# Two graph layers in one kernel: planned PSUM banks, and attention scores in clusters of four

## The chip, the cores and the metric

The kernel runs on one core of a Trainium2 chip. The metric is the device time of one execution in microseconds (us), the median of several runs. All arithmetic is float32. Engines are named as in the profile: PE is TensorE, DVE is VectorE, ACT is ScalarE, POOL is GpSimd, and SP is SyncE, whose queue issues nearly all DMAs.

## The reference

Two layers follow each other on 64 graphs of 256 nodes with 512 features. `adj` is the same 0/1 matrix in both.

```python
# layer 0
fp = x @ fc_w.T + fc_b
logits = (fp @ q_w.T + q_b) + swap(fp @ k_w.T + k_b)     # one number per pair of nodes
masked = logits + (1 - adj) * -1e9
masked = where(masked >= 0, masked, 0.01 * masked)
x = softmax(masked) @ fp + x
# layer 1, 8 heads of 64
Q, K, V = x @ W_q + b_q, x @ W_k + b_k, x @ W_v + b_v
scores = Q K^T / sqrt(64) + (x @ w_g[:D])[:, None] + (x @ w_g[D:])[None, :] + b_g + log(adj + 1e-9)
out = softmax(scores) @ V + x
```

## The kernel before

**Groups and steps.** Two graphs make a group: 512 nodes in four tiles of 128. There are 32 groups. `step(d, a, f, n, check)` runs once per group, and interleaves up to four groups at different stages: F (`f`) goes through layer 0 and the projections of layer 1, A (`a`, one group earlier) through the attention of layer 1, D (`d`, one earlier still) is finished and stored, and X (`n`, the next) is loaded. The schedule is written out by hand: strings such as `A("scores:2 attend:0 totals_0")` name methods of a group, and each method puts its instructions on the engines' queues in that order. Every engine works through its own queue in order, and waits by semaphore for what its operands need. In `attention_and_layer_0` (L1068) stands the first half of a step, in `step` (L1107) the second. The first group's layer 0 is computed on a path of its own (`features_first`), and the last step has no next group and runs the last group's attention too.

**Products.** Each projection (`pq`, `pk`, `pv`, and `pf` for layer 0) is a 2x2 block product with seven multiplications instead of eight, as in Strassen's scheme. `p1` to `p7` are those; each is four matmuls of 128x128 by 256 columns (`Product.add`, L401, matmul at L412), and the profile counts two instructions for a float32 matmul. Some open a PSUM bank (`fresh`: p1, p7, p2, and for `pf` p3), some add to one that stands (p6, p5, p3 to p1's; p4 to p7's). `keep_1` and others copy a bank to SBUF on ACT (L429, L432, L494), and `sum_00`, `sum_11`, `sum_10` add such a copy to a bank on DVE (L443, L501). So pk.p4 may add to its bank only when DVE has read it for pk.sum_11.

**Attention.** `scores:u` (L847) makes two blocks of scores, u being a graph of the group and half of its heads. A block is four matmuls with 64 rows each (L859); two of them use the upper and lower half of the array at the same time, and write two banks. One exponential on ACT reads both banks of the block, 1024 elements per partition (L873). `factor:u:jc` multiplies a block by the adjacency on DVE (L879), `both:u` adds the two blocks (L886), `parts:u` makes row sums of them. `attend:gr` (L888) multiplies the weights by V with 64 columns per matmul (L899), `totals` sums over partitions with a short matmul (L927). `turn`, `ratios`, `divide`, `complete`, `store` finish the output on DVE and send it off.

**Layer 0 and the loads.** `mix:c` (L689) multiplies x by the weights of layer 0. `send`/`fetch` bring the new x through DRAM into transposed form by one DMA out and four DMAs in; `xsum` (L375) and `copy` (L378) prepare sums and copies of its blocks. `keys:t` takes a dot product of each tile of x (L519, named `jc`); x has one buffer, so `load_x` for the next group can start only after that, and `dot_q`, `dot_k` (L519, `jq` and `jk`) wait for that load. `weights:jc` (L604 to L609) makes the next group's layer 0 weights.

**PSUM.** There are eight banks of 128x512 float32. Pool `ps` has four one-bank buffers that rotate over all uses (`bank(name)`), pool `psc` has two pairs of banks (`pair(name)`), for score blocks and for pq.p7. A tile waits until the last reader of the buffer that it gets is done.

Of the kernel before, what the change touches and what calls it, by code (L numbers as in the profile page):

```python
# [17 lines left out]
P = 128  # L18
# [7 lines left out]
def kernel(  # L26
# [118 lines left out]

    def transposed_weights(w, pool, psum, copy):

        t = pool.tile([P, NC, D], F32, tag="fcT", name="fcT")
        for hc in range(NC):
            pt = psum.tile([P, 512], F32, tag="bank", name=f"pfc_{hc}")  # L150
            for oc in range(NC):
                nc.tensor.transpose(pt[:, ts(oc, P)], w[:, oc, ts(hc, P)], ident)
            copy(t[:, hc, :], pt)
        return t
# [9 lines left out]
    def fast():  # L164
        main = ExitStack()
        with main:
# [5 lines left out]
            ps = main.enter_context(  # L172
                tc.tile_pool(name="ps", bufs=4, space=bass.MemoryType.PSUM)
            )
            psc = main.enter_context(
                tc.tile_pool(name="psc", bufs=2, space=bass.MemoryType.PSUM)
            )

            def bank(name):
                return ps.tile([P, 512], F32, tag="bank", name=name)  # L180

            def pair(name):
                return psc.tile([P, 2, 512], F32, tag="pair", name=name)

# [60 lines left out]
            def columns(rows, cols, name):  # L245

                n = rows.shape[0]
                pt = bank(name)
                nc.tensor.transpose(pt[:, 0:n], rows, ident[0:n, 0:n])
                nc.vector.tensor_copy(cols, pt[:, 0:n])  # L250
# [6 lines left out]
            def rows_of_x():  # L257

                pr = bank("rows_qk")[0:2, :]
                for oc in range(NC):  # L260
                    nc.tensor.matmul(
                        pr, lhsT=cols_0[:, oc : oc + NC + 1 : NC], rhs=fc_nat[:, oc, :],
                        start=(oc == 0), stop=(oc == NC - 1),
                    )
                rows = one.tile([2, D], F32, tag="junk", name="rows_qk_sb")
                nc.scalar.copy(rows, pr)
                return rows

            def spread_rows(rows):

                for n, dst in enumerate((wq_row, wk_row)):
                    pt = bank(f"row_{n}")
                    nc.tensor.matmul(
# [5 lines left out]
            def constant():  # L279
# [5 lines left out]
                nc.vector.tensor_reduce(part[:, 0, 0:1], both, AX.X, ALU.add)  # L285
                pk = bank("pk")
                nc.tensor.matmul(
# [7 lines left out]
            def constants_of_projections():  # L295


                pc = bank("pc")[:, 0:HALF]
                for c in range(NC):
# [10 lines left out]
                def add():  # L310
                    pt = bank("pct")
                    for m in range(2):
# [76 lines left out]
            class Product:  # L389
# [4 lines left out]

                scores = False

                def __init__(self, name, a, b, out, rows, bias=None):
                    self.name, self.a, self.b, self.out = name, a, b, out
                    self.rows, self.bias = rows, bias

# [16 lines left out]

                def fresh(self, n, scores=False):
                    name = f"{self.name}_{n}"
                    dst = (pair(name)[:, 0] if scores else bank(name)).rearrange(  # L420
                        "p (m k) -> p m k", m=2
                    )
                    self.add(n, dst, True)
                    return dst
# [36 lines left out]
                def p7(self):  # L461
                    self.r2 = self.fresh(7, self.scores)

# [65 lines left out]
            class Group:  # L529


                older = None

                def __init__(self, g):
# [42 lines left out]
                def queries(self):  # L577

                    pt = bank(f"qrow_{self.g}")
                    for t in range(T):  # L580
# [51 lines left out]
                def recip(self):  # L632

                    lo = ALL - TOK // B
                    first = lo if self.older is None else 0
                    all_sums = bank(f"rc_{self.g}")[:, 0:ALL]
                    nc.tensor.matmul(  # L637
# [14 lines left out]
                def sums(self):  # L652

                    sm = bank(f"sm0_{self.g}")[:, 0:P]
                    for jc in range(TPG):
# [9 lines left out]
                def recip_of_sums(self):  # L665
                    pt = bank(f"rc_{self.g}")[:, 0:P]
                    nc.tensor.transpose(pt, self.sms, ident)
# [4 lines left out]
                def mix(self, c):  # L672

                    g = self.g
                    if c == 0:
# [9 lines left out]
                        )  # L685
                    y = bank(f"y_{g}_{c}")
                    for gr in range(GP):
# [9 lines left out]
                def features_first(self):  # L697
# [4 lines left out]
                    for t in range(T):  # L702
                        pt = bank(f"xTp_{g}_{t}")
                        for c in range(NC):
# [4 lines left out]
                        if t == 0:  # L709
                            spread_rows(rows_qk)  # L710
                    fcT = transposed_weights(fc_nat, wts, ps, nc.scalar.copy)
                    for t in range(T):
                        self.dot_q(t)

                    def product(t):
                        pp = bank(f"fp_{g}_{t}")
                        for c in range(NC):
# [28 lines left out]
                    for t in range(T):  # L746
                        gr, ic = divmod(t, TPG)
                        po = bank(f"x1p_{g}_{t}")
                        for j in range(TPG):
# [15 lines left out]
                def begin(self):  # L765
# [18 lines left out]
                    self.pq = Product(f"pq_{g}", "q", b, to(self.qT), False, bq_col)  # L784
                    self.pq.scores = True
                    self.pk = Product(f"pk_{g}", "k", b, to(self.kT), False)
# [20 lines left out]
                def x1t(self, t):  # L807

                    pt = bank(f"x1Tp_{self.g}_{t}")
                    for c in range(NC):  # L810
# [36 lines left out]
                def scores(self, u):  # L847
# [5 lines left out]
                    for jc in range(TPG):  # L853
                        t = gr * TPG + jc
                        sc = pair(f"sc_{g}_{u}_{jc}").rearrange("p a (b i) -> p a b i", b=2)
                        for pr in range(2):
                            for par in range(2):
                                rows = slice(par * HD, (par + 1) * HD)
                                nc.tensor.matmul(  # L859
                                    sc[:, par, pr, :],  # L860
                                    lhsT=self.kT[rows, 2 * hg + pr, ts(t, P)],
# [9 lines left out]
                        else:  # L871
                            e = six.tile([P, 2, 2, N], F32, tag="e", name=f"e_{g}_{u}_{jc}")
                        nc.scalar.activation(e, sc, AF.Exp, bias=self.c[:, t : t + 1], scale=SCALE)  # L873
                        self.e[u, jc] = e
# [13 lines left out]
                def attend(self, gr):  # L888
# [3 lines left out]
                    for hg in range(2):  # L892
                        po = bank(f"oT_{g}_{gr}_{hg}")
                        oT = po.rearrange("p (r i) -> p r i", r=2)
# [39 lines left out]
                def totals_1(self):  # L934
                    self.totals(1, bank(f"tot_{self.g}_1")[:, 0 : NC * N // B])

                def totals_0(self):
                    self.totals(0, bank(f"tot_{self.g}_0")[:, 0 : NC * N // B])

# [15 lines left out]
                def sums_1(self, gr):  # L955

                    g = self.g

                    sm = bank(f"sm_{g}_{gr}")[:, 0:N]
                    for hg in range(2):  # L960
# [10 lines left out]
                def sums_of_e(self, gr):  # L971

                    g = self.g
                    sm = bank(f"sm_{g}_{gr}")[:, 0:N]
                    for hg in range(2):
# [92 lines left out]
            def attention_and_layer_0(D, A, F, X):  # L1068

                A("scores:0")  # L1070
                D("attend:1")
                F("add_tiles")
                A("scores:1 factor:0:0 factor:0:1 pv.sum_11 pv.p3 pv.p4")
                D("turn:1")
                F("parts_0")
                A("factor:1:0 factor:1:1 pv.sum_10 both:0 both:1")
                F("mix:0 mix:1 ysum:0 recip")
# [6 lines left out]
                F("pf.p7 pf.p5 pf.p3 pf.add_01 pf.sum_11 send:1:1")  # L1084
                A("scores:2 attend:0 totals_0")
                F("pf.sum_01 send:0:1 fetch:1:1 fetch:0:1")
                F("copy:0")
                A("factor:2:0 factor:2:1 scores:3 turn:0 ratios:0 both:2")
                F("pf.p4 pf.sum_10 send:1:0 fetch:1:0")
                F("pq.p1 pq.keep_1 pk.p1 pk.keep_1 pv.p1 pv.keep_1")  # L1090

            def check_ranges():

                in_range(NG - NR // 2, NG, "last")
                pk = bank("pok")
                nc.tensor.transpose(pk[0:1, 0:P], checked["all"], ident)
# [10 lines left out]
            def step(d, a, f, n, check):  # L1107
# [23 lines left out]
                F("xsum:0 xsum:1 xsum:2 pq.p6")  # L1131
                A("factor:3:0 factor:3:1 both:3")
                F("keys:2 keys:3 keys:0 keys:1")
# [16 lines left out]
                F("turn_residual:0")  # L1150
                if n is None:
                    A("attend:1 totals_1 ratios:1 turn:1 divide:1 complete:1 store:1")
                    F("residual:1 turn_residual:1")
# [16 lines left out]
            with tc.manual_schedule(engines=ENGINES):  # L1170
                f = Group(0)
                f.x, f.a = x_0, adj_0

                warm = bank("warm")
                for n in range(6):
# [16 lines left out]
    def general(pool):  # L1192
# [12 lines left out]
        with tc.tile_pool(name="gwps", bufs=2, space=bass.MemoryType.PSUM) as wps:  # L1205
            fcT = transposed_weights(fc_nat, pool, wps, nc.vector.tensor_copy)
        with tc.For_i(0, NG, 1) as g, ExitStack() as stack:
# [198 lines left out]
```

## Time and profile before

| | |
|---|---|
| Median of three runs | 2311.59 us (2310.92 to 2312.35) |
| Profiled execution, first to last instruction (its span) | 2308.8 us |
| Median less span | 2.8 us |
| Mean granted TensorE clock | 0.997 of full |
| PE instructions | 12618 |
| One steady step | 70.88 us |
| PE, DVE, ACT busy in one steady step (70.90 us window) | 70.90, 66.35, 33.42 us |

The profile gives the span of its one execution, and no other time of it. The median less the span is what lies around the instructions. A row of the profile's groups reads: line, engine, operation, output and inputs by name, shape, number of instructions, then busy time, mean duration in ns, and idle time before them. "64*128" at a matmul is the part of the array in use: rows by columns.

### The profile page before, as it was taken

To read this page: it belongs to the slowest core of one execution; us is meant where nothing else is said; L and a number is where in the kernel's file an instruction comes from. 1 tells how busy PE (TensorE), PEld (TensorE's weight loads), DVE (VectorE), ACT (ScalarE), POOL (GpSimd) and SP (SyncE) were. 2 spreads that over 40 slices of the span, in tenths; PEclk is the share of its full clock that TensorE was granted. 3 is DMA by queue.
4 is the path that set the end of the run, shared out by engine and by line. 5 is a ranking of instruction groups with operands and counts; after the bars stand their busy time and mean duration, and the time that the engine had idled before them with its cause. 6 is when DMAs were issued, how large, how long until landed. Compare 5 with 4: busy or idle time off the path is not lost.

```text
span 2308.8 us, 33613 instructions
## 1 busy us (share of the span) xinstructions
PE 2294.2 (99%) x12618; PEld 1905.2 (83%) x12618; DVE 2124.2 (92%) x3180; ACT 1071.8 (46%) x1865; POOL 121.9 (5%) x120
## 2 busy tenths in 40 slices
PE   9999999999999999999999999999999999999997
PEld 6888888888888888888888888888888888888885
DVE  6899999999999999999999999999999999999997
ACT  3544444454445444454444454444544445444443
POOL 0000000000000000000000000000000000000000
PEclk9999999999999999999999999999999999999999
DMA  4122332223322233232233232332222323223312
GB/s 133 46 61 73 78 76 66 70 61 85 79 73 61 61 78 78 74 68 61 69 78 83 60 75 63 79 78 74 64 60 74 78 73 70 65 64 81 84 46 38
DMA packets 517264, 163.84 MB, mean 71 GB/s; under 512 B 415188, under 2 KB 478696, under 8 KB 517096
## 3 DMA queue, kind: packets, MB, share of 16 engines
q1 hardware_dynamic: 514440, 160.32, 28.8%
q8 instruction: 102, 1.67, 0.3%
q10 hardware_dynamic: 2656, 1.31, 0.2%
q14 instruction: 66, 0.54, 0.1%
HBM read 95.43 MB, written 66.12 MB: 70 GB/s over the span
## 4 chain that ended last, share of the span: by engine, by line
PE 98%; DVE 1%; DMA 0%; ACT 0%; issue 0%; ACTq 0%; DVEq 0%
PE pv L412 17%; PE pq L412 17%; PE pf L412 16%; PE pk L412 16%; PE sc L859 11%; PE oT L899 10%; PE y L689 9%; PE fp L718 1%; DMA fc_nat<-in_L_gnn_fc_w_dram 0%; PE rc L637 0%; DVE osb L1034 0%; PE tot L927 0%; DVE osb L1040 0%; PE xTp L705 0%; DVE osb L1033 0%; DVE x L756 0%
## 5 line engine op out<-in xcount | busy, mean ns | idle before, releaser
L873 ACT ACTIVATE e<-sc,c 128x1024 f32<-128x1024 f32 x254 | 269.0, 1110 | 79.2 <-PE sc L859 77.6
L879 DVE TENSOR_TENSOR e<-e,am 128x1024 f32<-128x1024 f32 x254 | 297.7, 1213 | 0.4 <-ACT e L873 0.4
L859 PE MATMUL sc<-qT,kT 64*128 64x256 f32 x2048 | 255.8, 390 | 0.3 <-ACT e L873 0.3
L899 PE MATMUL oT<-e,v 128*64 128x256 f32 x2032 | 233.4, 382 | 0.0
L859 PEld LDWEIGHTS sc<-qT,kT 64*128 64x128 f32 x2048 | 187.3, 187 | 52.6 <-issue 32.7
L495 POOL TENSOR_TENSOR pf_s<-pf_s,x 128x512 f32<-128x512 f32 x93 | 118.4, 1273 | 2106.1 <-ACT pf_s L494 2038.8
L689 PE MATMUL y<-e,x 128*128 128x256 f32 x992 | 225.6, 381 | 0.0
L899 PEld LDWEIGHTS oT<-e,v 128*64 128x64 f32 x2032 | 140.2, 137 | 85.3 <-issue 10.7
L689 PEld LDWEIGHTS y<-e,x 128*128 128x128 f32 x992 | 186.4, 190 | 23.7
L432 ACT ACTIVATE pq_s<-pq,cols 128x256 f32<-128x256 f32 x192 | 80.5, 470 | 249.1 <-PE pq L412 249.1
L494 ACT ACTIVATE pf_s<-pf,recip 128x256 f32<-128x256 f32 x186 | 77.9, 470 | 197.6 <-PE pf L412 197.6
L917 DVE TENSOR_REDUCE part<-est 128x32 f32<-128x1024 f32 x124 | 151.3, 1220 | 4.3
L916 DVE STREAM_TRANSPOSE est<-es 128x1024 f32<-128x1024 f32 x124 | 152.2, 1227 | 0.0
L886 DVE TENSOR_TENSOR es<-e,e 128x1024 f32<-128x1024 f32 x126 | 149.3, 1205 | 1.1
L695 ACT COPY yT<-y 128x512 f32<-128x512 f32 x124 | 72.6, 585 | 131.7 <-PE y L689 130.9
L429 ACT COPY pk_s<-pk 128x512 f32<-128x512 f32 x96 | 56.3, 586 | 165.7 <-PE pk L412 159.0
L906 ACT COPY oTs<-oT 128x512 f32<-128x512 f32 x128 | 75.0, 586 | 118.0 <-PE oT L899 97.3
L412 PE MATMUL pk<-t1b,wk 128*128 128x256 f32 x512 | 121.1, 380 | 0.4 <-DVE kT L443 0.4
L412 PE MATMUL pv<-wv,t1b_c 128*128 128x256 f32 x512 | 121.1, 380 | 0.0
L412 PE MATMUL pv<-wv,t1b 128*128 128x256 f32 x512 | 121.0, 380 | 0.0
L412 PE MATMUL pq<-x1T,wq 128*128 128x256 f32 x512 | 121.0, 379 | 0.0
L412 PE MATMUL pk<-x1T,wk 128*128 128x256 f32 x512 | 121.0, 379 | 0.0
(181 smaller groups left out, 4506.3 us busy)
## 6 DMA issues: line engine op xcount, KB each, us to landing
x<-in_x_dram SPq DMA_DIRECT2D x32, 1024.0 KB, 5.1
out_dram<-osb SPq DMA_DIRECT2D x254, 128.0 KB, 3.1
xd<-xt SPq DMA_DIRECT2D x124, 256.0 KB, 2.0
x1T<-xd SPq DMA_DIRECT2D x496, 64.0 KB, 1.9
adj<-in_adj_dram SPq DMA_DIRECT2D x128, 128.0 KB, 3.5
qrow<-q SPq DMA_DIRECT2D x31, 256.0 KB, 3.9
fc_nat<-in_L_gnn_fc_w_dram ACTq DMA_DIRECT2D x4, 256.0 KB, 3.8
wq<-in_L_gnn_W_q_dram SPq DMA_DIRECT2D x1, 1024.0 KB
```

What stands on the lines that cost most here:

```text
L412: nc.tensor.matmul(o, lhsT=lk[:, ts(m, P)] if len(lk.shape) == 2 else lk[:, m], rhs=rk, start=(start and m == 0 and k == 0), stop=(m == 1 ...
L432: nc.scalar.activation(dst[:, m], src[:, m], AF.Identity, bias=self.bias[:, 2 * o + m : 2 * o + m + 1],)
L494: nc.scalar.mul(s[:, m], src[:, m], self.recip[:, TPG * k + m : TPG * k + m + 1])
L495: nc.gpsimd.tensor_tensor(s, s, self.out(o, k), ALU.add)
L689: nc.tensor.matmul(y[:, ts(gr, N)], lhsT=self.x[:, gr * TPG + j, ts(c, P)], rhs=self.e0[:, j, gr, :], start=(gr == 0 and j == 0), stop=(gr ...
L859: nc.tensor.matmul(sc[:, par, pr, :], lhsT=self.kT[rows, 2 * hg + pr, ts(t, P)], rhs=self.qT[rows, 2 * hg + pr, ts(gr, N)], start=True, st ...
L873: nc.scalar.activation(e, sc, AF.Exp, bias=self.c[:, t : t + 1], scale=SCALE)
L879: nc.vector.tensor_tensor(ef, ef, self.am[:, jc, u // 2, :].unsqueeze(1).to_broadcast([P, 4, N]), ALU.mult,)
L886: nc.vector.tensor_tensor(self.esum[u], self.e[u, 0], self.e[u, 1], ALU.add)
L899: nc.tensor.matmul(oT[par * HD : (par + 1) * HD, pr, :], lhsT=self.v[:, gr * TPG + jc, ts(h, HD)], rhs=self.e[2 * gr + hg, jc][:, par, pr, :],
L916: nc.vector.transpose(turned, self.esum[u].rearrange("p a b i -> p (a b i)"))
L917: nc.vector.tensor_reduce(self.part[:, hg, :], turned.rearrange("p (m c) -> p m c", c=B), AX.X, ALU.add,)
```

## The change

Eight PSUM tiles of one bank each, named Xa, Xb, Ya, Yb, Za, Zb, Wa and Wb, take the place of both pools. Every product of a projection gets a fixed slot. Score blocks of a step use pairs: Y, Z, W, Y for `scores:0` and `scores:1`, and X, Z, W, X for `scores:2` and `scores:3`; attention, totals and row sums have slots too. The last group keeps to Y and Z. What has no slot of its own takes seven of the banks in turn. The two banks of a block are now separate tiles, and each is read by an exponential of its own, 512 elements per partition.

The order of a step changes in `attention_and_layer_0`: `attend:1` of the older group goes ahead of `scores:0`, `scores:1` follows `scores:0` at once, and pf.p4 moves between `totals_0` and `scores:2`, with `scores:3` as the next matmuls. On VectorE, `parts_0` and the turning of outputs move with it, and `factor:2:0` is issued after the first products of pq, pk and pv; `factor:2:1` and `both:2` move into the second half of the step, behind the first three `xsum`.

```diff
+            banks = {
+                n + h: ps.tile([P, 512], F32, tag=f"bank_{n}{h}", name=f"bank_{n}{h}")
+                for n in "XYZW" for h in "ab"
+            }
+            FREE = ("Xa", "Xb", "Ya", "Yb", "Za", "Zb", "Wa")
+            def bank(slot=None):
+                if slot is None:
+                    turns[0] += 1
+                    slot = FREE[turns[0] % len(FREE)]
+                return banks[slot]
...
+                slots = dict(v="Xa Xb Wb", q="Ya Yb Wa", k="Za Zb Ya", fc="Xa Yb Xb Za")
...
+                score_pairs = "YZWYXZWX"
+                attend_slots = 2 * (("Wa", "Wb"),)
+                total_slots = ("Ya", "Zb")
+                sum_slots = ("Wb", "Xa")
...
-                        nc.scalar.activation(e, sc, AF.Exp, bias=self.c[:, t : t + 1], scale=SCALE)
+                        for par in range(2):
+                            nc.scalar.activation(
+                                e[:, par], sc[par], AF.Exp, bias=self.c[:, t : t + 1], scale=SCALE
+                            )
...
-                A("scores:0")
                 D("attend:1")
-                F("add_tiles")
-                A("scores:1 factor:0:0 factor:0:1 pv.sum_11 pv.p3 pv.p4")
+                F("add_tiles parts_0")
+                A("scores:0 scores:1 pv.sum_11")
                 D("turn:1")
-                F("parts_0")
-                A("factor:1:0 factor:1:1 pv.sum_10 both:0 both:1")
+                A("factor:0:0 factor:0:1 pv.p3 pv.p4 factor:1:0 both:0 factor:1:1 pv.sum_10 both:1")
...
-                A("scores:2 attend:0 totals_0")
+                A("attend:0 totals_0")
                 F("pf.sum_01 send:0:1 fetch:1:1 fetch:0:1")
-                F("copy:0")
-                A("factor:2:0 factor:2:1 scores:3 turn:0 ratios:0 both:2")
-                F("pf.p4 pf.sum_10 send:1:0 fetch:1:0")
+                F("pf.p4")
+                A("ratios:0 turn:0 scores:2")
+                F("pf.sum_10 send:1:0 fetch:1:0 copy:0")
+                A("scores:3")
                 F("pq.p1 pq.keep_1 pk.p1 pk.keep_1 pv.p1 pv.keep_1")
+                A("factor:2:0")
...
                 F("xsum:0 xsum:1 xsum:2 pq.p6")
-                A("factor:3:0 factor:3:1 both:3")
+                A("factor:2:1 both:2 factor:3:0 factor:3:1 both:3")
...
                 if n is None:
+                    f.score_pairs = 4 * "YZ"
+                    f.attend_slots = (("Wa", "Wb"), ("Ya", "Yb"))
+                    f.pv.slot[2] = "Xb"
```

## The prediction

> **What bounds the kernel now.** I read the page first: busy shares, then the chain that ended last.
>
> ```profile
> PE 2294.2 (99%) x12618; PEld 1905.2 (83%) x12618; DVE 2124.2 (92%) x3180; ACT 1071.8 (46%) x1865; POOL 121.9 (5%) x120
> PE 98%; DVE 1%; DMA 0%; ACT 0%; issue 0%; ACTq 0%; DVEq 0%
> ```
>
> TensorE is the wall: busy nearly throughout, and the chain never leaves it. VectorE comes second with 92%. A busy share can hide waits and slow issue, so next the table of waits, for TensorE alone; its rows end in total us, number, longest:
>
> ```profile
> PE pk L412 <- DVE kT L443: 0.4, 1, 0.4
> PE sc L859 <- ACT e L873: 0.3, 1, 0.3
> ```
>
> Outside start and end these are its only waits, one each. The chain in order of time repeats every 70.88 us in steady state. So buffers hold up almost nothing; what is left to win is how closely matmuls follow each other. The timeline of TensorE over one stretch of a step (start, duration, engine, line, operands):
>
> ```profile
> 1063.71 1.89 PE L412 MATMUL pv<-wv,t1b 128*128 128x256 f32 x8
> 1065.53 2.00 PE L859 MATMUL sc<-qT,kT 64*128 64x256 f32 x16
> 1067.45 3.67 PE L899 MATMUL oT<-e,v 128*64 128x256 f32 x32
> 1071.06 2.00 PE L859 MATMUL sc<-qT,kT 64*128 64x256 f32 x16
> 1072.99 1.99 PE L412 MATMUL pv<-v_s,t1b_c 128*128 128x256 f32 x8
> 1074.82 1.89 PE L412 MATMUL pv<-wv,t1b 128*128 128x256 f32 x8
> 1076.54 0.81 PE L689 MATMUL y<-e,x 128*128 128x256 f32 x3
> ```
>
> Take the starts. The undisturbed eight full matmuls last 1.72 us (1074.82 to 1076.54), 216 ns each. The eight just after scores last 1.83, the eight before scores 1.82. Sixteen score instructions run two at a time (64 of 128 rows each), so 8 x 216 ns = 1.73 is due, and 1.92 is taken. Thirty-two attention instructions, paired in columns, should take 3.45 and take 3.61. Each change of array shape (F full, R half the rows, C half the columns) costs something. Single starts show how much: the first instruction of a new shape comes 93 to 100 ns late, and the one after it, whose weights were not loaded ahead, 104 ns late into R or F and 51 ns into C. The sums are F to R 197 ns, R to C 148, C to R 204, R to F 201. F to C (143) occurs twice, in the last step. From the short totals matmul into F takes exactly what it takes into R (152 ns, then 320).
>
> **What the skill says.** "TensorEngine Tiling (Array Packing)", Key Properties: changing the tiling mode, not just the tile, drains TensorE. The trace agrees and prices it at 0.14 to 0.20 us. "TensorE: Matmul & The Clock Gate", Step-by-step: weight loads are pulled ahead of matmuls in flight. The trace agrees: inside a block the load starts with the matmul before it, 216 ns ahead. So a wait is felt 216 ns before its matmul, less 29 ns, since a load takes 187.
>
> **The change part by part.**
>
> *Order.* A steady step now has the shapes F R C R F, F R C R F: eight switches. Moving attend:1 ahead of scores:0, joining scores:0 to scores:1, and moving pf.p4 between totals and scores:2 with scores:3 behind it, gives F C R F, F C F R F: seven. Before: 197+148+204+201 and 197+148+201, with totals to R between. After: 143+204+201, 143+197+201, with totals to F at the same price. 1296 - 1089 = 207 ns per step. The first attention step has no attend:1 of an older group and gains nothing here; 30 steps x 0.207 = **-6.2 us**. Matmul count and sizes stay.
>
> *Banks in the first attention step.* There scores:0 and scores:1 already stand together, and the kernel before shows what four blocks cost with two pairs of banks:
>
> ```profile
> 76.22 2.00 PE L859 MATMUL sc<-qT,kT 64*128 64x256 f32 x16
> 77.40 2.12 ACT L873 ACTIVATE e<-sc,c 128x1024 f32<-128x1024 f32 x2
> 78.56 2.14 PE L859 MATMUL sc<-qT,kT 64*128 64x256 f32 x16 [0.35 <-ACT e L873]
> ```
>
> Block three starts at 78.56 instead of 78.05, after the first exponential; block four loses 0.04 more, and each restart 0.10. Three pairs with the fourth block back on the first take this away: **-0.7 us**, once.
>
> *Exponential in halves.* ScalarE rows give its price:
>
> ```profile
> L873 ACT ACTIVATE e<-sc,c 128x1024 f32<-128x1024 f32 x254 | 269.0, 1110 | 79.2 <-PE sc L859 77.6
> L432 ACT ACTIVATE pq_s<-pq,cols 128x256 f32<-128x256 f32 x192 | 80.5, 470 | 249.1 <-PE pq L412 249.1
> ```
>
> Between 256 and 1024 elements: 0.833 ns each and 257 ns fixed, so a half of 512 takes 683. Successive starts lie 98 ns less apart, 585, and 1012 for a whole. So 254 blocks cost 158 ns more each, 40 us on an engine idle for 1237: nothing by itself. It counts in the cluster. The first exponential starts 1.18 us after the cluster (77.40 - 76.22); the second half ends at 1.18 + 0.585 + 0.68 = 2.45, and a waiting weight load follows 0.05 later: 2.50. Block four starts at 0.32 + 11 x 0.216 = 2.69, its load is due at 2.48. So it is 0.02 us late, within the 29 ns of play. Bounds: 0, and a whole unprefetched load (104 ns) in 60 clusters, 6.2 us. I take **+0.3**; a gain below 0 is excluded, as that wait did not exist.
>
> *Moved vector work.* factor:2:0 now stands just after pq.p1 in issue order, and factor:2:1 and both:2 behind the first three xsum. Between pq.p1 and the last of the four key dots VectorE gains two operations of 1.134 us (factor:2:1, both:2): +2.27. It enters that stretch earlier: before, xsum:0 starts 1.58 us after pq.p1 (1105.25 against 1103.67); after, factor:2:0 ends where the cluster's exponentials allow: 2.50 + 1.13 = 3.63 after the cluster's start, and pq.p1 stands at 3.65. The dots come 2.27 - 1.60 = 0.67 us later against pq.p1. TensorE's way from there to pk.p4 is 0.10 longer (pq.p1 now follows R): net 0.57. This matters because load_x, issued on SP's queue, must wait for those dots to release x, and the next dots wait for the load:
>
> ```profile
> 1113.71 0.40 SPq L206 DMA_DIRECT2D x<-in_x_dram  x1
> 1118.90 0.69 DVE L519 CUSTOM_DVE_ANT_0 jq<-x,wq_row 128x512 f32<-128x512 f32 x1 [0.41 <-DMA x<-in_x_dram]
> ```
>
> VectorE goes on almost without a pause to pk.sum_11, which frees the bank of pk.p4. I took that margin from the trace in every step: end of kT's first sum to the first matmul of pk.p4 is 1.05 us in most (1126.55 to 1127.68), 0.55 in one, and 0.09 in the step whose load came latest:
>
> ```profile
> 772.45 0.68 DVE L443 TENSOR_TENSOR kT<-pk,pk_s 128x512 f32<-128x512 f32 x1
> 773.18 1.38 PEld L412 LDWEIGHTS pk<-t1b,wk 128*128 128x128 f32 x7 [0.20 <-DVE kT L443]
> ```
>
> About 0.24 is needed (0.05 for the semaphore, 0.19 for the load). 1.05 - 0.57 = 0.48 suffices; the two late steps would lose some 0.25 and 0.6, minus 0.07 lost already: **+0.8 us**, between 0.2 and 3, as landing times vary. Behind the waiting pk.p4 stand pv.p2, pv.p6 and the next attend.
>
> *The rest, at nothing.* pf.p4 comes earlier, so pf.sum_10, send:1:0 and its four fetch DMAs on SP's queue start some 3.5 us earlier against pq.p1; they were hidden and stay so. attend:1 comes 1.9 us earlier; its second bank (Wb) is freed by pv.sum_00, which ends at 1137.37 with that half due at about 1138.3: 0.9 us of cover; without it up to that lag per step. copy:0 now stands between two pairs of exponentials; pv.p1 needs it 7.1 us after the cluster's start, and it is done at about 4.2. turn:1, parts_0 and totals move within idle or non-critical time; POOL's sums keep place. Fixed slots replace rotation: each reuse in a step has an older reader with over 0.5 us to spare except the two above. The start rotates over seven banks instead of four: 0 to -0.4, taken as 0. In the last step the exponentials are done near 2285.7 and the last factor starts at 2288.69, so longer halves are covered.
>
> Sum: -6.2 - 0.7 + 0.3 + 0.8 = **-5.8 us**. The profiled span of 2308.8 becomes 2303.0. The median, 2311.59, holds 2.8 us more around the span, which stays: **2305.8 us**. A measurement of this kernel can tell about 0.2%, 4.6 us, from no change.
>
> **Rivals.**
> 1. *The fourth block of each cluster waits.* For: the computed margin is nil, and two fixed costs stand where one stood. Against: it needs the half to be longer than the line through two rows says. At 70 ns in 60 clusters +4.2: about 2309.7, inside no change.
> 2. *VectorE becomes the bound, slower.* If part of the 1.6 us head start is missing (exponentials late, or the moved multiplications not absorbed before the key dots), then dots, load, kT's sum and pk.p4 slip by that part in every step. It decides from 0.24 us of lag beyond mine; slower by 0.2% needs 0.6 (0.35 x 30 = 10.4 = 5.8 + 4.6). At 1.0: 0.76 x 30 = +23, about 2329. For: VectorE is 92% busy, and the late step proves the path. Against: it is idle for some 4.5 of the 70.88 us of a step, in several places.
> 3. *The joined clusters save no switch time* because the price hangs on something else, such as bank order. Only the first step's 0.7 would be left, less the losses: about 2312. Against: all kinds of switch show one price at every occurrence.
>
> **How the numbers follow.** My forecast has 0.72 (2303.8 to 2307), rival 1 0.15, rival 2 0.08, rival 3 0.05. Faster by over 0.2% (below 2306.97): 0.73, with a little of rival 1 in and the upper edge of my case out; within 0.2%: 0.18; slower: 0.09. The range takes in my case and most of rival 1: 2303.6 to 2310.0.
>
> **What would show it.** Right: steady step 70.67 instead of 70.88; score blocks of 32 instructions in a row; no TensorE wait on e in the first attention step; a half exponential near 683 ns. Wrong: many TensorE waits on e (rival 1) or on kT from VectorE (rival 2), or a step of 70.88 without waits (rival 3).

## The result, and the profile after

The changed kernel is slower. Its median is 2332.32 us (2330.81 to 2332.78, four runs), against 2311.68 (2310.92 to 2312.35, four runs) for the kernel before: a ratio of 1.0089, interval 1.0075 to 1.0104. That is 20.6 us more where the forecast had 5.8 less. The span of the profiled execution is 2330.2 us instead of 2308.8.

Busy time and chain of the page after:

```profile
PE 2303.7 (99%) x12618; PEld 1899.5 (82%) x12618; DVE 2134.1 (92%) x3180; ACT 1102.5 (47%) x2121; POOL 122.0 (5%) x120
...
PE 46%; DVE 36%; DMA 11%; SPq 3%; issue 3%; DVEq 0%; ACT 0%
```

The busy shares look as before. The chain does not: of the time on it, only 46% is TensorE's, where it had 98%. VectorE, a transfer and SP's queue carry the rest. PE's 99% is no contradiction. A float32 matmul of 256 columns counts as busy for 379 ns while the next starts 216 ns later, so the first 0.16 us of every gap stay hidden in the busy share.

The table of waits of the kernel after (engine, output, line, releaser: us in total, times, longest):

```profile
DVE jq L521 <- DMA x<-in_x_dram: 48.1, 30, 2.6
...
DVE t1b L379 <- DMA x1T<-xd: 26.6, 31, 2.4
...
PEld bank_Zb L417 <- DVE kT L445: 20.2, 29, 1.3
...
PEld bank_Wb L912 <- DVE v L445: 15.1, 30, 0.5
...
PE bank_Zb L417 <- DVE kT L445: 8.5, 16, 0.9
...
PE bank_Ya L417 <- ACT pq_s L434: 1.3, 2, 0.7
```

The weight loads of pk.p4 now wait for `kT` 29 times, in nearly every step. attend:1 has a new wait in every step, for `v`, and pq.p3 now and then waits for ScalarE's copy. Above them stand two waits of VectorE for transfers. The rows of the kernel before that answer to the first three:

```profile
DVE jq L519 <- DMA x<-in_x_dram: 14.2, 24, 1.5
...
PEld pk L412 <- DVE kT L443: 1.0, 2, 0.8
...
DVE t1b L375 <- DMA x1T<-xd: 0.4, 1, 0.4
```

So the new thing furthest upstream is that VectorE waits for **x1T**, the transposed x that `xsum` reads.

The starts of TensorE's matmuls give the bill. A steady step takes 71.56 us on average, 70.91 at least. In the version with both repairs, below, each takes 70.67, so 30 steps lose 26.6 us against it. Set beside it matmul by matmul, three places make up 21.3 of them: the first matmul of pk.p4 comes 12.8 us late in all (27 steps), attend:1's second bank 6.5 (30 steps), pq.p3 2.0 (5 steps). After such a gap the second matmul is late too, because its weights were not loaded ahead: 2.9, 1.5 and 0.5 us, 5.0 together. That is about 0.10 each time in shape F and 0.05 in C, the prices of the prediction. Some 0.3 us stays unassigned.

Of the 21.4 us by which the profiled span grew, the 30 steps hold 20.4. The first attention step became 0.9 shorter, the stretch before the first pq.p1 1.2 and that behind the last one 0.7 longer. A difference at the start says little: the first pq.p1 stands anywhere from 41.7 to 45.1 us in the profiled executions reported here, the last of them left out.

How one step runs into it, from the timeline of the kernel after (start, duration, engine, line, operands, idle time before in brackets; lines between left out):

```profile
1106.48 0.71 DVE L798 STREAM_TRANSPOSE xt<-x 128x512 f32<-128x512 f32 x1
...
1107.80 3.67 SPq L810 DMA_DIRECT2D x1T<-xd  x8
...
1111.38 1.23 DVE L892 TENSOR_TENSOR e<-e,am 128x1024 f32<-128x1024 f32 x1 [0.73 <-ACT e L884]
...
1112.58 1.99 PE L417 MATMUL bank_Ya<-x1T,wq 128*128 128x256 f32 x8
...
1113.35 0.69 DVE L379 TENSOR_TENSOR t1b<-x1T 128x512 f32<-128x512 f32 x1 [0.74 <-DMA x1T<-xd]
...
1124.25 0.40 SPq L210 DMA_DIRECT2D x<-in_x_dram  x1
...
1129.45 0.69 DVE L521 CUSTOM_DVE_ANT_0 jq<-x,wq_row 128x512 f32<-128x512 f32 x1 [1.79 <-DMA x<-in_x_dram]
...
1136.41 0.68 DVE L445 TENSOR_TENSOR kT<-bank_Zb,pk_s 128x512 f32<-128x512 f32 x1
```

pq.p1 starts at 1112.58. factor:2:0 ends at 1112.61, just as the prediction had it. But `xsum:0` does not start then: send:0:1 has turned the last piece of x at 1106.48, the last of eight fetches is issued by 1111.47, and xsum:0 must wait for x1T until 1113.35. Everything behind keeps that delay: key dots, load_x, dot_q, and kT's first sum, which ends at 1137.09.

Medians over 28 steps, in us after pq.p1's first matmul, from the starts in the traces. "Undone" is the changed kernel with factor:2:1 and both:2 put back, an experiment below:

| | before | after | undone |
|---|---|---|---|
| issue of fetch:0:1's last fetch ends | -1.15 | -1.12 | -1.13 |
| xsum:0 starts | 1.75 | 0.64 | 2.37 |
| last key dot ends | 10.06 | 11.39 | 10.72 |
| dot_q starts | 15.44 | 16.92 | 16.12 |
| kT's first sum ends | 23.09 | 24.57 | 23.77 |
| pk.p4 starts | 24.17 | 24.62 | 24.28 |

With no wait pk.p4 would start at 24.28 in the new order, and it needs 0.24 us after kT's sum, so the sum must end by 24.04. It ends at 24.57: **0.53 us late** in the median step. In the record pk.p4 then starts at 24.62, 0.34 late and only 0.05 behind the sum, because a matmul that had to wait is recorded as starting together with its weight load (1137.15 and 1137.14 in the step above). The second matmul loses the other 0.10.

### The profile page after: what moved, and what is told of

Its sections match the earlier page's. It is cut to its first block, busy times and chain, and to the rows that moved or that the text cites. A ratio compares the mean times of both kernels' runs of the same rounds, so it can differ in the third digit from the quotient of the medians.

```text
span 2330.2 us, 33775 instructions
## 1 busy us (share of the span) xinstructions
PE 2303.7 (99%) x12618; PEld 1899.5 (82%) x12618; DVE 2134.1 (92%) x3180; ACT 1102.5 (47%) x2121; POOL 122.0 (5%) x120
## 4 chain that ended last, share of the span: by engine, by line
PE 46%; DVE 36%; DMA 11%; SPq 3%; issue 3%; DVEq 0%; ACT 0%
PE bank_Xa L417 10%; DMA x<-in_x_dram 6%; PE bank_Xb L417 6%; DVE e L892 4%; SPq L810 3%; DVE jq L521 3%; PE bank_Wb L912 3%; DVE x L503 3%; DMA xd<-xt 3%; DVE es L899 3%; PE bank_Ya L869 3%; DVE est L929 3%; PE bank_Wa L695 2%; PE bank_Zb L695 2%; PE bank_Za L695 2%
## 5 line engine op out<-in xcount | busy, mean ns | idle before, releaser
L496 ACT ACTIVATE pf_s<-bank_Xa,recip 128x256 f32<-128x256 f32 x186 | 78.0, 470 | 197.6 <-PE bank_Xa L417 197.6
L434 ACT ACTIVATE pq_s<-bank_Ya,cols 128x256 f32<-128x256 f32 x192 | 82.0, 489 | 181.0 <-PE bank_Ya L417 131.4
L521 DVE CUSTOM_DVE_ANT_0 jq<-x,wq_row 128x512 f32<-128x512 f32 x128 | 88.5, 692 | 51.4 <-DMA x<-in_x_dram 48.1
L912 PE MATMUL bank_Wa<-e,v 128*64 128x256 f32 x1008 | 122.7, 385 | 0.0
L912 PE MATMUL bank_Wb<-e,v 128*64 128x256 f32 x1008 | 121.0, 382 | 1.4
L835 ACT ACTIVATE xv<-x1T,cols 128x256 f32<-128x256 f32 x256 | 109.0, 498 | 2.1 <-DVE osb L1004 1.3
L521 DVE CUSTOM_DVE_ANT_0 jk<-x,wk_row,kqc 128x512 f32<-128x512 f32 x128 | 95.4, 745 | 2.5
L798 DVE STREAM_TRANSPOSE xt<-x 128x512 f32<-128x512 f32 x124 | 88.3, 712 | 4.3
L521 DVE CUSTOM_DVE_ANT_0 jc<-x,wgc_row 128x512 f32<-128x512 f32 x128 | 88.3, 690 | 3.3
L610 DVE SCALAR_TENSOR_TENSOR e<-qrow,kq,e 128x256 f32<-128x256 f32 x128 | 80.7, 675 | 0.1
```

Source lines behind the costliest of these rows:

```text
L521: nc.vector.tensor_tensor_reduce(out=junk, in0=src, in1=w_row, scale=1.0, scalar=init, op0=ALU.mult, op1=ALU.add, accum_out=dst,)
L798: nc.vector.transpose(xt.rearrange("p (q n m) -> p n q m", q=P // B, m=B), x1)
L835: nc.scalar.activation(self.xv[:, c].rearrange("p (t a m) -> p t a m", t=TPG, m=B), self.x1T[:, c // 2, gr].rearrange("p (a t c m) -> p c ...
L912: nc.tensor.matmul(oT[par * HD : (par + 1) * HD, pr, :], lhsT=self.v[:, gr * TPG + jc, ts(h, HD)], rhs=self.e[2 * gr + hg, jc][:, par, pr, :],
```

## The experiments

The theory: VectorE's chain (x1T, xsum, the two moved operations, key dots, load_x, dot_q, kT) has become the bound, and the banks and clusters themselves give what was forecast. The rivals: the clusters save nothing, the fourth block of a cluster or the two exponentials delay TensorE, or the fixed bank slots cost the time.

### The move alone, in the kernel before

```diff
-                A("factor:2:0 factor:2:1 scores:3 turn:0 ratios:0 both:2")
+                A("factor:2:0 scores:3 turn:0 ratios:0")
...
-                A("factor:3:0 factor:3:1 both:3")
+                A("factor:2:1 both:2 factor:3:0 factor:3:1 both:3")
```

> The kernel before, with nothing changed but factor:2:1 and both:2 moved behind the first three xsum, ahead of the key dots. Theory V: xsum:0 cannot start earlier (pf.sum_10 and send:1:0 stand ahead of it and wait for pf.p4), so the key dots come the full 2.27 us later; of that 0.8 us is margin at pk.p4, so up to 1.4 us per step is lost, 2340 to 2355. Rival N or a rival that blames banks, clusters or halves: no change, 2311 to 2313.

Measured: 2356.9 us, ratio 1.0197 (1.0181 to 1.0213), a little above the range that was expected. Its waits:

```profile
PEld pk L412 <- DVE kT L443: 38.5, 31, 1.6
...
PE pk L412 <- DVE kT L443: 26.0, 31, 1.2
...
PEld pq L412 <- ACT pq_s L432: 16.6, 31, 1.5
```

With the old banks, whole exponentials and old order of scores, this one move brings the same wait on `kT`. xsum:0 stands at 1.75 as before, and the key dots end 2.39 us later, so the two operations cost 2.39. The kT sum ends 2.42 later; the margin was 1.08 - 0.24 = 0.84, so 1.58 per step is due, and the step grew by 72.43 - 70.88 = 1.55. The path and its arithmetic hold. Some 0.4 of the 1.55 are lost before pk.p4, at pq.p3, which now waits for ScalarE's copy in every step. Without the new order there is no head start to soften it, which is why it is worse than the whole change.

### The move undone in the changed kernel

```diff
-                A("factor:2:0")
+                A("factor:2:0 factor:2:1 both:2")
...
-                A("factor:2:1 both:2 factor:3:0 factor:3:1 both:3")
+                A("factor:3:0 factor:3:1 both:3")
```

> The changed kernel, with factor:2:1 and both:2 put back behind factor:2:0, ahead of xsum:0. Theory V: the two operations fill the time in which VectorE waited for x1T (0.74 us), so the key dots come about 0.9 us earlier than in the changed kernel, roughly where the prediction had put them; a few waits on kT are left, 2306 to 2310. Rival N (not these two operations but the new place of attend:1, turn:1 and parts_0 makes VectorE late): 2328 or more.

Measured: 2306.31 us, ratio 0.9976 (0.9966 to 0.9986). Twenty-six of the 30 steps take 70.67 us. One takes 72.94, behind a load that landed 2.4 us later than usual, and three lose 0.6 us together. xsum:0 now starts at 2.37, behind two more operations, and never waits for x1T. Yet the key dots end 0.67 *earlier* than in the changed kernel, at 10.72, where the prediction had put them (10.06 + 0.67). The fixed slots and two exponentials are all in this kernel, so they are not what costs.

### The key dots and the load first

In the changed kernel, and the same in the kernel before:

```diff
-                A("factor:2:1 both:2 factor:3:0 factor:3:1 both:3")
                 F("keys:2 keys:3 keys:0 keys:1")
                 X("load_x")
+                A("factor:2:1 both:2 factor:3:0 factor:3:1 both:3")
```

> The changed kernel, with the four key dots and load_x of the next group issued ahead of the five moved vector operations (factor:2:1, both:2, factor:3:0, factor:3:1, both:3) instead of behind them. Theory V (vector chain: the moved operations delay the key dots, hence the load of x, hence kT's first sum and pk.p4, and then pv.sum_00 and the second bank of attend:1): the load is issued about 5 us earlier, TensorE's waits on kT and on v vanish, a steady step is 70.67 us, and the total is 2304 to 2306.5. Rival D (VectorE waits 0.74 us for the DMA into x1T before xsum:0, and that wait itself is what TensorE pays for): that wait is untouched, and most of the slowdown stays, 2320 or more. Rival W (VectorE has too much to do in any order): 2325 or more.

Measured: 2307.18 us, ratio 0.9983 (0.9976 to 0.9989), just above the range of theory V and far below those of its rivals. VectorE still waits 23.8 us for x1T here, in 31 waits, against 26.6 in the changed kernel, so that wait by itself is not what TensorE pays for. The load leaves 6 us earlier (5.49 against 11.53 after pq.p1), and pk.p4 waits for kT only in the last step, as in the kernel before. In its place, in five steps, pq.p3 comes 2.3 us late in all, waiting for ScalarE's copy, which waits for a sum that now stands on VectorE behind the five postponed operations. The steps average 70.81 us: some 4 us are lost in place of 27. The lateness has moved to another reader, at a small part of the price.

> The kernel before, with the key dots and load_x issued ahead of factor:3:0, factor:3:1 and both:3. Theory V: the kernel before has only one wait on this chain in 30 steps (0.07 us), so nothing is to be won: 2311 to 2312. A rival in which the order of the key dots is worth something by itself (fewer collisions of DMAs, say): faster by several us.

In the kernel before: 2311.38 us, ratio 0.9998 (0.9989 to 1.0006), all steps 70.88. An earlier load is worth nothing where nothing waits for it, so the gain in the changed kernel is the wait removed.

### Both, the best version

The move undone, and the keys and load_x ahead of factor:3:0, factor:3:1 and both:3.

> The changed kernel with both repairs: factor:2:1 and both:2 back ahead of xsum:0, and the key dots and load_x ahead of factor:3:0, factor:3:1 and both:3. Theory V: the load comes early and nothing of pq's sums is pushed back, so the last waits of the two single repairs go as well. 30 steps of 70.67 us instead of 70.88 and no wait in the first attention step: 7 us under the kernel before, 2304 to 2305.5. Rival: what is left in the single repairs comes from landing times that no order takes away: 2306 to 2308.

Measured: **2303.05 us**, ratio 0.9965 (0.9951 to 0.9978), span 2301.3. That is a little below the range that was expected. Both kernels are beaten, and the changed one by 29 us. Against the single repairs the intervals of the ratios overlap; that both together are better is shown by the steps, not by the times. All of TensorE's waits that have a releaser, in this kernel's table of waits for PE:

```profile
PE bank_Za L1109 <- DVE okp_last L1078: 4.9, 1, 4.9
PE bank_Xb L1192 <- POOL ones L218: 1.5, 1, 1.5
PE bank_Yb L816 <- DVE x L762: 0.5, 1, 0.5
PE bank_Zb L417 <- DVE kT L445: 0.4, 1, 0.4
PE bank_Yb L265 <- DVE cols L254: 0.3, 1, 0.3
```

They belong to start and end; the one on kT stands in the last step, where the kernel before has it too. Every steady step takes 70.67 us. No row names the exponentials `e`: two clusters of four, three pairs of banks and the halves cost TensorE nothing.

### One cluster split again

In that best version scores:1 goes between pv.p3 and pv.p4, which are both F: two more changes of shape per step.

```diff
-                A("scores:0 scores:1 pv.sum_11")
+                A("scores:0 pv.sum_11")
...
-                A("factor:0:0 factor:0:1 pv.p3 pv.p4 factor:1:0 both:0 factor:1:1 pv.sum_10 both:1")
+                A("factor:0:0 factor:0:1 pv.p3 scores:1 pv.p4 factor:1:0 both:0 factor:1:1 pv.sum_10 both:1")
```

> The kernel with both repairs, with scores:1 moved from the end of the first cluster to between pv.p3 and pv.p4: two more shape switches per step (R to F, F to R), nothing else but the order of the exponentials. If a switch costs what the prediction says (201 + 197 ns), 30 steps lose 11.9 us: 2316 to 2318. If clusters are worth nothing by themselves: 2304 to 2306. More than 2320 would mean that later exponentials delay VectorE.

Measured: 2315.78 us, ratio to the kernel before 1.0022 (1.0012 to 1.0032). The time is 12.7 us above the version with both repairs, for 11.9 expected, and each steady step takes 71.07, 0.40 more. F to R and R to F cost 0.197 + 0.201 = 0.398 by the prices read from the kernel before. The rival that the clusters save nothing is out.

### Why x1T is late

The first try moves only fetch:1:1, whose DMAs stand ahead of fetch:0:1 on SP's queue, to POOL's.

```diff
-                        nc.sync.dma_start(dst[q], src[q])
+                        (nc.gpsimd if (o, k) == (1, 1) else nc.sync).dma_start(dst[q], src[q])
```

> The changed kernel, with the four DMAs of fetch:1:1 issued on POOL's queue instead of SP's, ahead of fetch:0:1's four. On SP eight such issues take 3.67 us. Theory V with SP's issue time as the reason why VectorE waits for x1T before xsum:0: that wait of 0.74 us goes, key dots and load come that much earlier, and most of the waits on kT with it: 2306 to 2318. If the wait is for the DMA's own transfer or for send:0:1 itself, not for SP: unchanged, 2328 to 2334.

Measured: 2332.06 us, ratio 1.0091 (1.0075 to 1.0106): no change. The timeline of this run around one pq.p1:

```profile
1105.75 2.17 POOL L810 DMA_DIRECT2D x1T<-xd  x4 [4.52 <-DMA xd<-xt]
...
1106.64 1.75 SPq L810 DMA_DIRECT2D x1T<-xd  x4
...
1109.93 1.99 PE L417 MATMUL bank_Ya<-x1T,wq 128*128 128x256 f32 x8
...
1110.76 0.69 DVE L379 TENSOR_TENSOR t1b<-x1T 128x512 f32<-128x512 f32 x1 [0.79 <-DMA xd<-xt]
```

SP is free for fetch:0:1 now, but its first DMA must wait until send:0:1 has landed, and four issues still follow one another to 1108.39. In the median step they end at -1.56 after pq.p1, 0.44 us earlier than in the changed kernel. That gains nothing, because the last fetch on SP now takes 2.7 us from the start of its issue to its landing, where it took 2.0: it lands at 0.68 instead of 0.50 (medians of the 19 landings that each trace holds). Why it lands more slowly was not tested; the fetches of both queues are now under way at the same time. In the second try each of the two sets is shared between the queues, two DMAs each.

```diff
-                        nc.sync.dma_start(dst[q], src[q])
+                        (nc.gpsimd if (k == 1 and q % 2) else nc.sync).dma_start(dst[q], src[q])
```

> The changed kernel, with the eight fetches of fetch:1:1 and fetch:0:1 shared between two queues: every second one goes to POOL's queue instead of SP's. In the run with only fetch:1:1 on POOL, the four fetches of fetch:0:1 still followed one another on SP for 1.75 us after send:0:1 had landed. If the issue of the last set is the link of the chain send:0:1, fetch:0:1, xsum:0 that can be shortened, its last fetch is issued 0.6 to 0.9 us earlier against pq.p1, VectorE's wait for x1T (26.6 us in 31 times) falls below 10 us, xsum:0 starts within 0.3 us of pq.p1, the key dots come about 0.6 earlier, pk.p4 is 0.53 - 0.6 short of nothing, and the time is 2306 to 2318 us. If what counts is the landing (POOL's fetches took 2.6 us to land where SP's took 2.0), most of the wait stays, and so does the time: 2328 to 2333 us.

Measured: 2317.86 us, ratio 1.0026 (1.0014 to 1.0037), with factor:2:1 and both:2 where the change put them. Its waits:

```profile
DVE t1b L379 <- DMA x1T<-xd: 12.5, 9, 3.1
...
PEld bank_Zb L417 <- DVE kT L445: 8.7, 11, 1.3
...
PE bank_Zb L417 <- DVE kT L445: 4.4, 9, 0.9
```

VectorE's wait for x1T falls from 31 times to nine, not quite to the 10 us expected, and in the median step xsum:0 starts at 0.06. Seventeen of 29 steady steps take 70.67 to 70.69. On average it is 71.09, so some 12 us are still lost. The last of the eight fetches, on POOL, is issued by -1.85, 0.72 us earlier than in the changed kernel; it takes 2.3 us to land, and so lands 0.5 us earlier, at -0.03. The link that could be shortened was the issue of the last fetches one after another, and part of what that saves is lost again in the landing. "DMA: Bandwidth & Descriptors" of the Trainium skill, section "Rules for kernel authors", says that spreading DMAs over queues brings no bandwidth and only saves issue time. This run agrees as to issue time, 0.44 us for each fetch on SP: sharing it took 14 us off the kernel, because the last DMA of the set is waited for. Why nine steps still get x1T late was not followed up.

### A pair of banks as one tile

On the best version, each pair becomes one tile of two banks, read by one exponential of 1024.

```diff
-                n + h: ps.tile([P, 512], F32, tag=f"bank_{n}{h}", name=f"bank_{n}{h}")
+                n: ps.tile([P, 2, 512], F32, tag=f"bank_{n}", name=f"bank_{n}") for n in "XYZW"
...
```

> The kernel with both repairs, with a pair of banks as one tile and one exponential of 1024 elements per block again, in the same order. ScalarE saves about 0.16 us per block, which lies beside other work; the fourth block's bank comes free at 2.34 us of the cluster instead of 2.50. If halves cost nothing on the path: within 1 us of the kernel with both repairs. If the late second half costs TensorE something (rival 1 of the prediction): 1 to 6 us faster than it.

Measured: 2698.92 us, ratio 1.1681 (1.1665 to 1.1697). The table of waits for PE begins:

```profile
PE bank_W L695 <- ACT yT L701: 49.7, 31, 1.6
PE bank_W L913 <- ACT oTs L920: 44.7, 63, 0.8
PE bank_Y L417 <- ACT pq_s L434: 29.7, 32, 0.9
```

The expected range was missed by far, and as a measurement of the halves the run is inconclusive. A matmul into one bank of a pair now waits for readers of the other (pf.p2 into Xb, for example, for the copy `pf_s` of Xa), in all 12 us in every step, and that drowns all else. What it does show is why the pairs had to be split into one-bank tiles once projections share them.

## Why the prediction was wrong, point by point

- **Order, -6.2: right.** 70.88 became 70.67 wherever nothing waits, and splitting a cluster again gave 0.40 for 0.398.
- **First attention step, -0.7: right.** TensorE's wait on `e` there is gone, and from the first pq.p1 to the second it is 66.97 us instead of 67.84. These 0.87 hold all that changed in that step.
- **Exponential in halves, +0.3: nothing was lost.** Rows of the kernel after by shape (minimum, median, maximum in ns):

```profile
L884 ACT ACTIVATE e<-bank_Ya,c x65: 663/687/723, 78.5 to 2299.5; 128x512 f32<-128x512 f32 x65
L884 ACT ACTIVATE e<-bank_Yb,c x65: 666/680/732, 79.1 to 2300.1; 128x512 f32<-128x512 f32 x65
```

  The estimate was 683, and the fourth block fits into the margin. Rival 1 is out.
- **Moved vector work, +0.8: this failed**, in the step "it enters that stretch earlier", the head start of 1.60 us. factor:2:0 did end at pq.p1. But xsum:0 needs x1T as well as a free VectorE, and the prediction never laid out when x1T lands. It could have: in the kernel before the last fetch lands at +0.4 (median of the 19 landings in its trace), and in the kernel after xsum:0 starts 0.12 us behind such a landing. The old start at 1.75 hid that; a start at 0 cannot. An estimate from these numbers is a head start of some 1.2, key dots 1.1 later, and 1.0 net, more than the margin of 0.84 (1.08 less the 0.24 needed).

  Measured, the head start was 1.75 - 0.64 = 1.11, and from xsum:0 to the last key dot it took 2.44 more instead of 2.27. So the dots came 1.33 later instead of 0.67. The wait for load x added 0.15, and kT's sum was 1.48 late, 1.37 net of TensorE's 0.11, where 0.57 net was forecast and 0.84 was to be had. That is the 0.53 us by which the sum comes late.

  Two readings were off besides, neither of them decisive. 1.58 is the distance from pq.p1's start in the chain (1103.67) to a start in the timeline, where pq.p1 stands at 1103.50, so 1.75 was due. And the margin is not 1.05 in most steps but runs from 0.74 to 1.27, the two late ones apart, with 1.08 between the medians; the pair of times given with it is 1.13 apart.

  The Trainium skill's "DMA: Bandwidth & Descriptors", section "Anatomy of one DMA — SWDGE (gpsimd) path", gives a DMA issued from GpSimd a fixed 2.0 us, most of it waiting for the receipt of the write. These fetches went on SP, which that section does not cover; the page of the kernel after shows 2.0 us for SP's fetches of 64 KB, and 2.0 also for its sends of 256 KB. So a smaller fetch would hardly have landed sooner, though that was not tried.
- **Four fetch DMAs that "were hidden and stay so":** said of send:1:0 and fetch:1:0, and true of them, though they start 2.6 us earlier against pq.p1 (1.26 instead of 3.89), not 3.5. The set that counted was the one before, fetch:0:1, which the prediction did not name.
- **attend:1's second bank, at nothing: wrong.** Of the 0.9 us of cover about 0.2 belongs to semaphore and weight load. pv.sum_00 ends 1.45 us later after pq.p1 than in the version with both repairs (35.36 against 33.91), and TensorE, held up by 0.44 at pk.p4, does not come late enough to hide that. It cost 6.5 us, and 1.5 more at the second matmul. In the best version the wait is gone.
- **Rival 2 is what happened**, as it said, "part of the 1.6 us head start is missing", though for neither of the two reasons that it gave in brackets, but for x1T. Measured beyond the forecast lag: 1.37 - 0.57 = 0.80, for which its formula gives 2305.8 + 30 x (0.80 - 0.24) = 2322.6. The time is higher because it left out attend:1's bank (6.5), pq.p3 (2.0) and the second matmuls whose weights were not loaded ahead (5.0); pk.p4's first matmul by itself cost less, 12.8 instead of 16.8. The rival got a small chance because VectorE's idle time, some 4.5 us of a step, counted as a reason against. Idle time elsewhere in the step is no help to a chain with its own transfers.

## What to carry to other kernels

When work is moved so that a chain may start sooner, look up every operand of its first instruction, transfers included, and when each lands; the head start ends at the latest. A margin of a microsecond between two engines belongs to all changes together: here 0.84 us of slack decided between 5 us won, with the move undone, and 21 lost. When a good reordering comes out slower, undo its parts one at a time before it is given up.

## What the runs showed of the hardware beyond that

The price of a change of array shape adds up exactly: seven, eight and nine changes gave steps of 70.67, 70.88 and 71.07 us, each kind at the price read in the kernel before. POOL's queue took 0.54 us to issue a fetch (2.17 for four) where SP's took 0.44 (1.75), and the page gave 2.4 us to landing for those on POOL in the run with shared queues, against 2.0 on SP.
